# Layer 2 of a four-layer model: the context product once a sequence, two groups' maxima turned over together, and filler work dealt out by matmul passes

## The chip, the cores and the metric

The kernel runs on one core of one Trainium2 chip. The metric is the device time of one execution in microseconds (us), as the median of the runs; lower is better. The changed lines all belong to layer 2 (and to the constants packed for it); layers 0, 1 and 3 keep their code.

## The reference, cut to what matters

Activations are `x`, 8 sequences (B) of 512 tokens (T) of 128 channels (C), float32. Each layer computes `x = x + attn(LN(x)) * silu(ffn(LN(x)))`. Layer 2 is:

```
# attention side, per sequence
qkv   = LN(xn; g_attn, b_attn) @ qkv_w + qkv_b          # 16 heads of width 8
attn  = causal softmax attention(q, k, v)
attn  = attn @ out_w + out_b
x     = xn + attn
ctx   = attn
xs, vs = LN(x; g1, b1), 0
for _ in range(8):                                       # NUM_ITERS
    u  = tanh(ctx @ w_ctx + xs @ w_x + b_inl)
    vs = vs + 0.1 * (u - xs - vs)
    xs = xs + 0.1 * vs
x = x + xs
h = gelu(LN(x; g2, b2) @ ff_w1 + ff_b1)
s = x + (h @ ff_w2 + ff_b2)
# ffn side, per sequence
h = silu(xn @ w1) * (xn @ w2)
h = gelu(h @ h1);  h = gelu(h @ h2)                      # 512 x 512 each
g = h @ w3
# together
x = x + s * silu(g)
```

`ctx @ w_ctx` does not change over the eight iterations.

## The kernel before

Data stand in SBUF with 128 rows. A tile of 128x512 holds one sequence, either by tokens or by features. Products over a whole sequence are matmuls of 128x128 weights and 512 columns in float32; one such product is called a *pass* here.

Layer 2 walks over 128 *units*: 8 sequences, 4 head groups `g` in each, and 4 key chunks `kc` of 128 keys (`JT = 4`). A group has four heads. It lies on four 32-row strips, so that its four narrow matmuls go to different strips of the array. A sequence is 16 units. For one unit there are three pieces of attention work:

- **W**, `weights`: the scores of one key chunk against the queries from that chunk on (512, 384, 256 or 128 columns for `kc` = 0 to 3), into two PSUM tiles `pu` of two banks each, and their exponential on ScalarE (ACT) into `at`, two heads to an instruction (L1411).
- **M**, `maxima`: the row maxima of the scores of one query tile, which are needed some units later. The same two `pu` tiles take the scores, four bf16 products with `ident_b` and `neg_b` add the causal mask (L1390), and VectorE (DVE) reduces them (L1393) into `mpad`. `put_maxima` turns a whole group's maxima over with four transposes and adds them into `qT` (L1400, L1401), where a column of -1 in the keys subtracts them from the scores.
- **S**, `sums`: two units later (`LAG`), the product of the exponentials with the values, into the single `pf` bank (L1424).

Both W and M use both `pu` tiles, so W, exponentials, M, reductions and the next W follow one another.

Between these pieces the loop of `layer2` deals out other work, as generators whose steps end at each `yield`. *Front* is what the next sequence needs: `begin` (layer norm, projections to q, k, v) and `ffn` (the whole ffn side: four steps of two passes for w1 and w2 at L1348 and L1349, one step of 16 passes for h1, one of 16 for h2, both at L1361 with a Gelu on ACT for each four passes at L1362, and w3 at L1368). *Back* is what the finished groups need: `group` (transposing and normalising a group's output, L1438; after the last group the output projection and `ctx`), then `rest` (layer norm, eight iterations with two passes each at L1474 and L1475, Tanh at L1477, updates of the state at L1479 to L1482, layer norm, the 512-wide feed-forward at L1498 and L1504). A step is taken at fixed places:

```
held[u] = L.weights(*units[u])
next(back, None)
...
next(front, None)
if u + AHEAD < len(units):
    L.maxima(*units[u + AHEAD])
next(back if u % 2 else front, None)
```

The maxima run `AHEAD = 5` units ahead. The order of TensorE (PE) is the order in which the code issues its work (`manual_schedule`); the other engines' orders are set by the framework's scheduler. All evacuations of front and back go through three one-bank PSUM tiles `pa`.

The functions the change touches, with those that call them:

Of the kernel before, what the change touches and what calls it, by code (L numbers as in the profile page):

```python
# [10 lines left out]
F32 = mybir.dt.float32  # L11
# [1158 lines left out]
def pack2(i):  # L1170
# [10 lines left out]
    p.add("own", one)  # L1181
    bq, bk = (strips2(b[None, n * C : (n + 1) * C]).reshape(2, P).T for n in range(2))
# [4 lines left out]
    bk[16::32] = -1.0  # L1187
    p.add("bk", bk)
# [58 lines left out]
class Layer2(BySequence):  # L1247
# [39 lines left out]
    def begin(self, b):  # L1287

        k, nc, cn, tp = self.k, self.k.nc, self.cn, self.tp
# [13 lines left out]
        yield  # L1303
        q["xT"] = tp.tile([P, T], F32, name="xT2", bufs=1)
        k.to_features(xn, q["xT"], nt=JT)
        yield
# [4 lines left out]
        yield  # L1311
        q["qT"] = tp.tile([P, 4, T], F32, name="qT2")
        q["kT"] = tp.tile([P, 2, T], F32, name="kT2")
        for t in range(2):
# [13 lines left out]
            yield  # L1328
# [8 lines left out]
        yield  # L1337

    def ffn(self, b):
# [5 lines left out]
        for o in range(4):  # L1345
# [8 lines left out]
            yield  # L1354
        for n in ("h1", "h2"):
            src, hA = hA, hid()
            for o in range(4):
                ps = k.pa()
                for i in range(4):
                    c0 = i * FF2 + o * P  # L1360
                    nc.tensor.matmul(ps, fn[n][:, c0 : c0 + P], src[:, i, :], start=(i == 0), stop=(i == 3))  # L1361
                nc.scalar.activation(hA[:, o, :], ps, AF.Gelu, scale=fn[n + "_s"][:, o : o + 1])  # L1362
            yield
# [9 lines left out]
        yield  # L1373
# [7 lines left out]
    def maxima(self, b, g, qt):  # L1381
        k, nc, q = self.k, self.k.nc, self.q[b]
        qT, kT = q["qT"][:, g, :], q["kT"][:, g // 2, :]
# [7 lines left out]
        for i, pu in pairs:  # L1391
            top = self.mpad[g % 2][:, qt, :].rearrange("p (i c) -> p i c", c=32)
            nc.vector.tensor_reduce(top[:, i : i + 2, 16], pu[:, :, 0:m], AX.X, ALU.max)  # L1393

    def put_maxima(self, b, g):

        k, nc, qT = self.k, self.k.nc, self.q[b]["qT"][:, g, :]
        ps = k.pa((P, JT, P))
        for t in range(JT):
            nc.tensor.transpose(ps[:, t, :], self.mpad[g % 2][:, t, :], k.ident)  # L1400
        nc.vector.tensor_tensor(qT, qT, ps.rearrange("p a b -> p (a b)"), ALU.add)  # L1401
# [30 lines left out]
    def group(self, b, g):  # L1432
# [11 lines left out]
        yield  # L1444
# [4 lines left out]
        yield  # L1449
# [6 lines left out]
        q["ctx"] = tp.tile([P, T], F32, name="ctx2")  # L1456
        nc.scalar.activation(q["ctx"], ps, AF.Identity, bias=self.out_bc, scale=100.0)
        yield

    def rest(self, b):  # L1460
# [6 lines left out]
        yield  # L1467
        yield
        k.to_features(h, X[0], nt=JT, scale=self.g1[:, 0:1], bias=self.g1[:, 1:2])
        yield  # L1470
        for it in range(ITERS):
            now, then = X[it % 2], X[1 - it % 2]
            ps = k.pa()
            nc.tensor.matmul(ps, cn["w_ctx"], q["ctx"], start=True, stop=False)  # L1474
            nc.tensor.matmul(ps, cn["w_x"], now, start=False, stop=True)  # L1475
            u = tp.tile([P, T], F32, name="u2")
            nc.scalar.activation(u, ps, AF.Tanh, bias=cn["b_inl"], scale=0.01)  # L1477
# [5 lines left out]
            yield  # L1483
# [6 lines left out]
        yield  # L1490
        yield
        k.to_features(h, hT, nt=JT, scale=cn["g2"], bias=cn["b2"])
        nc.gpsimd.tensor_tensor(xn, xn, bc(cn["ff_b2"], 1, JT), ALU.add)
        yield
# [5 lines left out]
        yield  # L1500
# [16 lines left out]
        yield  # L1517


def layer2(k, x, A, at):  # L1520

    with ExitStack() as ctx:
# [7 lines left out]
        AHEAD = JT + 1  # L1530
        for u in range(AHEAD):
            L.maxima(*units[u])
        for _ in L.ffn(0):
            pass
        L.put_maxima(0, 0)
        U = 4 * JT
        front = back = iter(())
        for u in range(len(units) + LAG):
# [3 lines left out]
            next(back, None)  # L1542
            if n == 1 and b + 1 < B:
                front = chain(L.begin(b + 1), L.ffn(b + 1))
            if u % JT == JT - 1 and u + 1 < len(units):
                L.put_maxima(*units[u + 1][0:2])
            next(front, None)
            if u + AHEAD < len(units):
                L.maxima(*units[u + AHEAD])
            next(back if u % 2 else front, None)  # L1550
            if u >= LAG:
                wb, g, kc = units[u - LAG]
                L.sums(wb, g, kc, held.pop(u - LAG))
                if kc == JT - 1:
                    back = chain(L.group(wb, g), back)
                    if g == 3:
                        back = chain(back, L.rest(wb))
        for _ in back:
            pass
# [574 lines left out]
```

## Time and profile before

| what | value |
|---|---|
| median of 3 runs | 3675.19 us (3669.09 to 3679.26) |
| the profiled execution | 3659.7 us, of which the span from first to last instruction is 3658.0 us |
| mean granted TensorE clock | 0.831 |
| PE busy in the span | 2812.2 us (77%) |
| DVE, ACT, POOL busy | 2265.6 us (62%), 1643.1 us (45%), 783.7 us (21%) |
| layer 2, from its first layer norm to the last work of its last sequence | about 1472 to 2653 us of the span |

A profile row names the line, engine, operation, output and inputs, how often it occurs, busy time and mean duration, and the idle time of the engine just before it with what ended that. PE records of a float32 product come in two halves, so 64 records of L1361 are 32 passes. "PEclk" is the share of its full clock that TensorE was granted. Matmul durations contain the time in the pipeline, so that back-to-back matmuls overlap in the record.

### The profile page before, as it was taken

The numbers are of one execution on the slowest core, as the hardware profiler recorded it, in microseconds if no ns is written. First come the engines' busy times: TensorE is split into PE (matmuls) and PEld (weight loads), VectorE is DVE, ScalarE is ACT, GpSimd is POOL, SyncE is SP. The second block draws the span as 40 slices with busy tenths as digits, with TensorE's granted clock in tenths as the row PEclk, the third lists the DMA queues.
The fourth block names the chain that finished last, engine by engine and source line by source line (L and its number), as shares of the span: only waits on it lengthen the run. The fifth ranks groups of instructions, "written<-read, shape, count | busy, mean of one in ns | idle before, by whom it ended". The sixth has DMA issues, their size and how long they took to land.

```text
span 3658.0 us, 45079 instructions
## 1 busy us (share of the span) xinstructions
PE 2812.2 (77%) x16390; PEld 1510.1 (41%) x16390; DVE 2265.6 (62%) x6274; ACT 1643.1 (45%) x3211; POOL 783.7 (21%) x915
## 2 busy tenths in 40 slices
PE   6164657512988888699999999998668789887987
PEld 4142445302444444344444444444344445444543
DVE  7989898997581121334445445444467777777775
ACT  5163546512544445233333333333245566666665
POOL 0004040400226664201101101101122222222220
PEclk8585757555899999799998998998878899888987
DMA  4002030311002221100000000000000000000000
GB/s 119 2 2 71 1 81 1 72 48 34 1 10 45 38 38 24 58 1 1 1 1 1 1 1 1 1 1 1 18 3 1 4 4 1 4 4 4 1 4 6
DMA packets 67519, 64.53 MB, mean 18 GB/s; under 512 B 5344, under 2 KB 59616, under 8 KB 66784
## 3 DMA queue, kind: packets, MB, share of 16 engines
q1 hardware_dynamic: 39264, 42.75, 3.7%
q0 software_dynamic: 19712, 14.69, 2.9%
q10 hardware_dynamic: 8320, 4.19, 0.4%
q8 instruction: 129, 2.11, 0.2%
q14 instruction: 94, 0.77, 0.1%
HBM read 43.80 MB, written 17.83 MB: 17 GB/s over the span
## 4 chain that ended last, share of the span: by engine, by line
PE 45%; DVE 32%; ACT 13%; POOL 4%; issue 3%; DMA 1%; ACTq 0%; POOLq 0%; SPq 0%; DVEq 0%
PE pa L1361 6%; PE pu L1379 6%; DVE nm L1949 4%; ACT at L1950 4%; PE pu L1066 2%; PE pf L1086 2%; PE pu L1946 2%; DVE mpad L1393 2%; PE pf L1424 2%; DVE Z L700 2%; PE pf L1931 1%; PE pa L1475 1%; PE pa L1474 1%; PE pa L1000 1%; DVE Z L706 1%
## 5 line engine op out<-in xcount | busy, mean ns | idle before, releaser
L1950 ACT ACTIVATE at<-pu,nm 128x512 f32<-128x512 f32 x512 | 347.7, 687 | 145.9 <-DVE nm L1949 115.6
L199 POOL TENSOR_SCALAR_AFFINE_SELECT at<-at 128x512 f32<-128x512 f32 x256 | 187.2, 751 | 1030.4 <-ACT at L1411 856.9
L1949 DVE TENSOR_REDUCE nm<-pu 128x1 f32<-128x512 f32 x512 | 326.4, 679 | 66.8 <-PE pu L1946 66.7
L1393 DVE TENSOR_REDUCE mpad<-pu 128x2 f32<-128x256 f32 (+3 forms) x256 | 199.0, 817 | 169.1 <-PE pu L1390 169.1
L1411 ACT ACTIVATE at<-pu 128x1024 f32<-128x1024 f32 (+3 forms) x256 | 171.6, 701 | 286.3 <-PE pu L1379 286.1
L1071 ACT ACTIVATE at<-pu,rsqrt 128x1024 f32<-128x1024 f32 (+3 forms) x256 | 190.4, 791 | 225.3 <-PE pu L1066 221.8
L1946 PE MATMUL pu<-qT,kT 32*128 32x512 f32 x1024 | 247.6, 700 | 6.4 <-ACT at L1950 5.4
L1361 PE MATMUL pa<-hid,f 128*128 128x512 f32 x512 | 222.7, 593 | 0.0
L1379 PE MATMUL pu<-qT,kT 32*128 32x512 f32 (+3 forms) x1024 | 161.4, 518 | 56.5 <-DVE mpad L1393 41.8
L748 PE MATMUL pa<-ident,Y 128*128 128x128 f32 x32 | 7.9, 424 | 216.3 <-DVE Y L739 216.3
L1379 PE MATMUL pu<-kT,qT 32*128 32x128 f32 (+3 forms) x1024 | 152.1, 571 | 14.3 <-ACT at L1411 10.2
L548 POOL DMA_INDIRECT xg<-xn_d,idx x48 | 53.1, 1106 | 503.9 <-PE pf L552 321.8
L1931 PE MATMUL pf<-at,va 128*32 128x512 f32 x1024 | 156.4, 687 | 1.4 <-POOL va L1924 1.4
L1361 PEld LDWEIGHTS pa<-hid,f 128*128 128x128 f32 x512 | 96.6, 190 | 119.5 <-issue 118.9
L1086 PE MATMUL pf<-at,va 128*32 128x512 f32 (+3 forms) x1024 | 106.1, 490 | 42.1 <-POOL at L199 41.8
L1482 DVE SCALAR_TENSOR_TENSOR X<-X,u 128x512 f32<-128x512 f32 x56 | 38.6, 690 | 159.5 <-ACT u L1477 159.5
L1066 PE MATMUL pu<-qT,kT 32*128 32x512 f32 (+3 forms) x1024 | 130.5, 520 | 5.9 <-ACT at L1071 4.9
L1924 POOL TENSOR_TENSOR va<-V,sm 128x32 f32<-128x32 f32 x128 | 38.4, 300 | 450.4 <-DVE sm L1923 399.7
L1379 PEld LDWEIGHTS pu<-qT,kT 32*128 32x128 f32 x1024 | 67.8, 198 | 155.1 <-DVE mpad L1393 115.6
L1946 PEld LDWEIGHTS pu<-qT,kT 32*128 32x128 f32 x1024 | 82.2, 208 | 103.2 <-ACT at L1950 65.5
L1009 POOL DMA_INDIRECT f_d<-ys,idx x64 | 101.2, 1582 | 95.7 <-DMA f_d<-ys,idx 51.4
L1362 ACT ACTIVATE hid<-pa,f 128x512 f32<-128x512 f32 x64 | 44.0, 687 | 172.6 <-PE pa L1361 172.6
(608 smaller groups left out, 6606.4 us busy)
## 6 DMA issues: line engine op xcount, KB each, us to landing
w<-in_w_dram SPq DMA_DIRECT2D x24, 512.0 KB, 3.3
f_d<-zeros ACTq DMA_DIRECT2D x8, 512.0 KB, 6.0
xn_d<-xn SPq DMA_DIRECT2D x8, 512.0 KB, 3.6
w<-in_w_dram SPq DMA_DIRECT2D x16, 256.0 KB, 2.8
w<-in_w_dram SPq DMA_DIRECT2D x24, 128.0 KB, 2.1
f<-in_f_dram SPq DMA_DIRECT2D x1, 2888.0 KB, 11.8
xn<-in_x_dram SPq DMA_DIRECT2D x4, 512.0 KB, 7.5
Gt<-in_x_dram SPq DMA_DIRECT2D x4, 512.0 KB, 3.9
```

The source lines that it names most:

```text
L199: self.nc.gpsimd.affine_select(a, a if src is None else src, pattern, ALU.is_ge, 0.0, base=0, channel_multiplier=-1)
L1066: nc.tensor.matmul(pu[:, n, 0:m], q["kT"][r, g // 2, kc * P : kc * P + P], q["qT"][r, g, kc * P :], start=True, stop=True,)
L1071: nc.scalar.activation(at_[:, i : i + 2, 0:m], pu[:, :, 0:m], AF.Square, bias=k.rsqrt2, scale=32.0**-0.5)
L1086: nc.tensor.matmul(po[i * 32 : i * 32 + 32, kc * P :], va[:, kc, c0 : c0 + 32], at_[:, i, 0 : T - kc * P], start=(kc == 0), stop=(kc == JT ...
L1361: nc.tensor.matmul(ps, fn[n][:, c0 : c0 + P], src[:, i, :], start=(i == 0), stop=(i == 3))
L1379: self.k.nc.tensor.matmul(pu[:, n, 0:m], a[r, c0 : c0 + P], b[r, q0 : q0 + m], start=True, stop=stop)
L1393: nc.vector.tensor_reduce(top[:, i : i + 2, 16], pu[:, :, 0:m], AX.X, ALU.max)
L1411: nc.scalar.activation(at_[:, i : i + 2, 0:m], pu[:, :, 0:m], AF.Exp, scale=8.0**-0.5)
L1931: nc.tensor.matmul(po[i * 32 : i * 32 + 32, :], va[:, kc, c0 : c0 + 32], E[:, i, :], start=(kc == 0), stop=(kc == JT - 1))
L1946: nc.tensor.matmul(pu, q["kT"][r, kc * P : (kc + 1) * P], q["qT"][r, g, :], start=True, stop=True)
L1949: nc.vector.tensor_reduce(nm[:, w], pu, AX.X, ALU.max, negate=True)
L1950: nc.scalar.activation(E[:, n, :], pu, AF.Exp, bias=nm[:, w], accum_out=sm[:, w])
```

## The change

It does five things.

1. `ctx @ w_ctx` is made once a sequence, in a new last step of `group`, and copied to SBUF by ACT. An iteration multiplies by `w_x` alone; DVE adds the stored product to the PSUM result, into `u`, and the Tanh then reads `u`.
2. Maxima of two groups share one `mpad` tile: the second group's go to the next column (17). `put_maxima` works once for two groups: four transposes, then for each group one DVE operation that multiplies by a new 0/1 column (`put`) and adds to that group's `qT`. The keys get a second column of -1.
3. Maxima run nine units ahead (`AHEAD = PAIR + 1`), and take the query tile `(n - 1) % JT` for unit index `n`, so that M's width grows over a group while W's shrinks.
4. Every step of front and back says how many passes it holds (`yield 4.0`). h1 and h2 give up their turn after each four passes rather than after sixteen. A new function `fill`, called twice a unit, takes one step of back and then as many steps of front as a budget allows: 1.8 passes a call in the first sequence, 2.43 later. `begin` of the next sequence goes ahead of what is left of the present one's `ffn`.
5. S comes directly after W, ahead of both fills; and the first sequence's `ffn` is dealt out between the first nine maxima.

```diff
     def ffn(self, b):
...
                 nc.scalar.activation(hA[:, o, :], ps, AF.Gelu, scale=fn[n + "_s"][:, o : o + 1])
-            yield
+                yield 4.0
...
     def maxima(self, b, g, qt):
...
-            top = self.mpad[g % 2][:, qt, :].rearrange("p (i c) -> p i c", c=32)
-            nc.vector.tensor_reduce(top[:, i : i + 2, 16], pu[:, :, 0:m], AX.X, ALU.max)
+            top = self.mpad[g // 2][:, qt, :].rearrange("p (i c) -> p i c", c=32)
+            nc.vector.tensor_reduce(top[:, i : i + 2, 16 + g % 2], pu[:, :, 0:m], AX.X, ALU.max)
...
-    def put_maxima(self, b, g):
+    def put_maxima(self, b, t):
...
-        for t in range(JT):
-            nc.tensor.transpose(ps[:, t, :], self.mpad[g % 2][:, t, :], k.ident)
-        nc.vector.tensor_tensor(qT, qT, ps.rearrange("p a b -> p (a b)"), ALU.add)
+        for qt in range(JT):
+            nc.tensor.transpose(ps[:, qt, :], self.mpad[t][:, qt, :], k.ident)
+        top = ps.rearrange("p a b -> p (a b)")
+        for v in range(2):
+            to = qT[:, 2 * t + v, :]
+            nc.vector.scalar_tensor_tensor(to, top, put[:, v : v + 1], to, ALU.mult, ALU.add)
...
     def group(self, b, g):
...
-        q["ctx"] = tp.tile([P, T], F32, name="ctx2")
-        nc.scalar.activation(q["ctx"], ps, AF.Identity, bias=self.out_bc, scale=100.0)
-        yield
+        ctx = tp.tile([P, T], F32, name="ctx2", bufs=1)
+        nc.scalar.activation(ctx, ps, AF.Identity, bias=self.out_bc, scale=100.0)
+        yield 2.25
+        ps = k.pa()
+        nc.tensor.matmul(ps, cn["w_ctx"], ctx, start=True, stop=True)
+        q["ctx"] = tp.tile([P, T], F32, name="cw2")
+        nc.scalar.copy(q["ctx"], ps)
+        yield 1.0
...
     def rest(self, b):
...
-            nc.tensor.matmul(ps, cn["w_ctx"], q["ctx"], start=True, stop=False)
-            nc.tensor.matmul(ps, cn["w_x"], now, start=False, stop=True)
+            nc.tensor.matmul(ps, cn["w_x"], now, start=True, stop=True)
             u = tp.tile([P, T], F32, name="u2")
-            nc.scalar.activation(u, ps, AF.Tanh, bias=cn["b_inl"], scale=0.01)
+            nc.vector.tensor_tensor(u, ps, q["ctx"], ALU.add)
+            nc.scalar.activation(u, u, AF.Tanh, bias=cn["b_inl"], scale=0.01)
...
 def layer2(k, x, A, at):
...
-        AHEAD = JT + 1
+        U = 4 * JT
+        PAIR = 2 * JT
+        AHEAD = PAIR + 1
+        HALF = (1.8, 2.43)
...
+        def fill():
+
+            nonlocal credit
+            half = HALF[u >= U]
+            credit = min(credit, half) + half - next(back, 0.0)
+            while credit > 0.0:
+                passes = next(front, None)
+                if passes is None:
+                    break
+                credit -= passes
+
         for u in range(len(units) + LAG):
             b, n = divmod(u, U)
             if u < len(units):
                 held[u] = L.weights(*units[u])
-            next(back, None)
-            if n == 1 and b + 1 < B:
-                front = chain(L.begin(b + 1), L.ffn(b + 1))
-            if u % JT == JT - 1 and u + 1 < len(units):
-                L.put_maxima(*units[u + 1][0:2])
-            next(front, None)
-            if u + AHEAD < len(units):
-                L.maxima(*units[u + AHEAD])
-            next(back if u % 2 else front, None)
+                if u % PAIR == PAIR - 1 and u + 1 < len(units):
+                    L.put_maxima(units[u + 1][0], units[u + 1][1] // 2)
             if u >= LAG:
                 wb, g, kc = units[u - LAG]
                 L.sums(wb, g, kc, held.pop(u - LAG))
...
+            if n == LAG - 1 and b + 1 < B:
+                front = chain(L.begin(b + 1), front, L.ffn(b + 1))
+            fill()
+            if u + AHEAD < len(units):
+                maxima(u + AHEAD)
+            fill()
```

## The prediction

> **What bounds the kernel now.** The profiled execution took 3659.7 us (3658.0 of span), 15.5 under the median of the runs; sums are made on it and carried to the median. First the page's slices: layer 2 lies in slices 17 to 29.
>
> ```profile
> PE   6164657512988888699999999998668789887987
> ...
> DVE  7989898997581121334445445444467777777775
> ...
> PEclk8585757555899999799998998998878899888987
> ```
>
> PE reads 9 of 10 there and DVE 3 to 5. Then the table of stretches: one steady sequence (columns: length, PE, PEld, DVE, ACT, POOL busy, clock), the unit that holds h1 and h2, and two thin stretches.
>
> ```profile
> 1804.10:1941.20 137.10, 128.66 (x717) 61.16 (x716) 65.15 (x105) 50.15 (x73) 18.26 (x23) 0.94 0.00 1
> ...
> 1860.50:1893.60 33.10, 33.10 (x100) 14.27 (x100) 2.93 (x5) 10.59 (x14) 0.63 (x1) 1.00 0.00 1
> 1920.48:1930.72 10.24, 8.32 (x50) 3.40 (x48) 6.82 (x14) 2.30 (x4) 3.37 (x4) 0.67 0.00 0
> 1944.94:1958.59 13.65, 10.87 (x56) 5.23 (x52) 7.98 (x17) 4.02 (x6) 6.29 (x6) 0.59 0.01 1
> ```
>
> PE looks 94% busy. The chain of waits corrects that: h1's 16 passes (32 records) take 13.73 us.
>
> ```profile
> 1862.28 13.73 PE pa L1361 x32
> ```
>
> A pass is therefore 0.858 us. Counting a sequence's work in passes by columns (front 50, back 30, W, M and S 10, 11 and 10, turned maxima 2; four strips count as one) gives 113, or 97 us of 137. The other 40 go to waits along W, exponential, M, reduction, W, and to about 20 us a sequence at half clock in units with little to fill. The exponentials' starts (L1411) show it: of the third sequence's units (counted from 0), 8 took 33.1 us with all of h1 and h2, 4 to 7 and 9 to 12 took 4.4 to 8.5; units 1, 13 and 14, with 1.8 to 3.1 passes in all, took 6.2 to 7.2.
>
> The waits of that sequence confirm it:
>
> ```profile
> PEld pu L1379 <- DVE mpad L1393: 15.0, 17, 1.9
> ...
> PEld pu L1379 <- ACT at L1411: 6.4, 12, 1.0
> ```
>
> **The change, part by part: what goes.** Of 64 context products 56 go: 56 x 0.858 = 48 us of PE. Of 128 maxima transposes 64 go, an eighth of a pass each: 7 us. DVE's operations for the maxima keep number and size (32 at 682 ns). The constants' load grows by 1 KB on SP's queue, long before use: nothing. POOL's selects and powers keep their number.
>
> **What comes.** 64 DVE additions of 128x512 from PSUM (nearest row: L1401, 682 ns) are 44 us of an engine that is under half busy; they matter only inside the iteration. And ACT changes table more often. The built order of ACT holds 143 table loads before and 233 after: 44 more ahead of h1's and h2's Gelus, one ahead of the 512-wide feed-forward's, and 45 more ahead of exponentials, because Gelus and exponentials now alternate. The timeline shows what one costs:
>
> ```profile
> 1937.98 0.69 ACT L1499 ACTIVATE hid<-pa,c 128x512 f32<-128x512 f32 x1 [0.17 <-PE pa L1498]
> 1939.88 1.28 ACT L1411 ACT_TABLE_LOAD   x1 [1.21 <-PE pu L1379]
> 1941.17 1.02 ACT L1411 ACTIVATE at<-pu 128x1024 f32<-128x1024 f32 x1
> ```
>
> The load to exponentials doesn't run in the 1.21 us that ACT idles: it stands behind the wait for W, so 1.28 us go between W and its exponentials, then to M (which needs `pu`). The load to Gelu starts at once and hides behind its four passes. So of 115 us of loads (90 x 1.283) the exponentials' half, 58 us, can be exposed, where less than about 1.5 us are dealt between W and M.
>
> Here the Trainium skill speaks against the change: "ScalarE: Activation LUTs" (Table sets: the hidden batching unit) says to batch calls by table set, and its section on the cost of a load counts 1283 ns plus a drain of 1380 ns for each switch. The trace agrees on the load and shows no drain (0.01 us to the exponential). With the page's 2.66 us the 45 exposed at most would be an estimated 120 us.
>
> **A unit, by rows.** W takes 1.14, 0.93, 0.71, 0.50 us for chunks 0 to 3, its two exponentials 2.04, 1.62, 1.20, 0.76, the reductions 0.42, 0.68, 0.95, 1.22 each (maxima widths run opposite now), the mask 0.4, S 1.06 to 0.43. From a W to the next W: M starts when both the dealt passes and the exponentials are done; the next W when both the second fill and the first reduction are. Each evacuation that a following product needs stalls it 0.7 to 0.8. On units 4 to 12 of the third sequence of before the rule gives 5.6, 5.4, 7.6, 8.5, 32.7, 10.3, 4.3, 7.0, 4.8 = 86.2 us; the trace has 86.0.
>
> I lay the new order out the same way for its fourth sequence (97 passes). Three of its units: the first has nothing between W and M and a load: 1.14 + 0.1 + 1.28 + 1.8 + 0.1 to M, 0.65 for M and mask, then four passes of h2, 3.5: 8.6. The seventh holds two iterations and two passes of w1/w2: it waits for the chain (below): 9.0. The thirteenth holds nothing and a load: 5.7. All sixteen: 8.6, 5.4, 6.6, 7.9, 8.6, 4.7, 9.0, 8.0, 8.0, 8.0, 10.2, 10.3, 5.7, 7.2, 7.5, 8.6 = 124.3. Of the seven loads to exponentials in them five lie open. Four of the six steady sequences hold 101 passes: 4 x 0.858 x 4/6 = 2.3 more, 126.6. Before, these six took 824.4 us, 137.4 each. So 10.8 x 6 = **-65 us**.
>
> **Half clock.** The rule assumes full clock. Before, the half clock set in around units whose passes fill 22 to 39% of their time (1.8 passes in 7.2 us, 3.1 in 6.7). New holes of that kind: the units with no fill and a load on chunk 0 leave PE idle 2.5 us; one or two a sequence. The step then dealt, up to four passes, takes up to 3.4 us more. I take 2 us a sequence, **+12**, from bounds of 0 and 7 (two steps).
>
> **First and last parts.** First sequence: 111 by the rule against 116.5: **-5**. Ahead of it, nine maxima between the ffn's steps in place of five alone: bare maxima took 14 us for five, the ffn 42; the new stretch is 51 passes, 44 us, with some 6 for cold start and stalls: 50 plus the W against 56: **-4** (0 to -9). Last sequence to its last S: it takes over some 30 passes of ffn that earlier ones leave, 99 us by the rule, against 99.6: **0** (-6 to +8). The tail runs the last iterations alone, and there the change costs. Before:
>
> ```profile
> 2620.54 1.13 PE L1475 MATMUL pa<-X,c 128*128 128x512 f32 x2 [0.65 <-DVE X L1482]
> 2621.51 1.02 PE L1474 MATMUL pa<-ctx,c 128*128 128x512 f32 x2
> 2621.71 0.69 ACT L1477 ACTIVATE u<-pa,c 128x512 f32<-128x512 f32 x1 [1.94 <-PE pa L1475]
> 2622.43 0.69 DVE L1482 SCALAR_TENSOR_TENSOR X<-X,u 128x512 f32<-128x512 f32 x1 [1.14 <-ACT u L1477]
> ```
>
> The context product ran behind Tanh, at no cost to the period of 2.63 us. The addition stands in the chain: +0.75 (0.69 and a handover), 3.38. And PE's share falls from 65% to 25%, among the shares that went cold before: at half clock the product takes 1.91 rather than 1.13 us (it did at 2606.6), a period of 4.2. So +6 to +12, taken near the cold end by those shares: **+10**.
>
> "TensorE: Matmul & The Clock Gate" (Why this matters for your kernels) warns of gaps of over some 3 us between bursts; the gaps here would be about 2.2, so by its letter the clock holds and the sum is 4 us lower. No row shows a lone product in such a period.
>
> In the steady part the same chain is 2.3 us without handovers between product and product; two iterations a unit, with exponentials and reductions of the same unit in the same in-order queues: behind the addition's wait on DVE stand the reductions that release `pu`, for which W waits; behind Tanh the exponentials. That is in the 9.0 and 8.0s above. If every one of the 64 waited 1 us more it would be +64: the upper bound; the lower is nothing.
>
> Sum: -65 + 12 - 5 - 4 + 0 + 10 = **-52** us; 3675 - 52 = 3623, taken as **3625**.
>
> **Rivals.**
> *The waits eat the gain.* All exponentials' loads open (two more a sequence, 2.6 us) and 0.5 us for each iteration: 8 x 2.6 = 21 and 64 x 0.5 = 32, which leaves +1: 3676. For it: ACT and DVE are strictly in order. Against: h-steps dealt between W and M cover the loads.
> *Slower, by the clock.* The dealt-out steps meet holes again and again: if PE runs 20 us a sequence at half clock as before, but now in units filled with passes, each loses half of that, 10 us: 8 x 10 = 80 instead of 12; -52 + 68 = +16: 3691. It decides from about 18 us a sequence at half clock. For it: 56 passes of filler are gone and loads open holes; against: units without passes were the cold ones, and now nearly every unit has some.
> *PE nearly full.* Every unit as the dense ones of before, 1.6 us and 0.858 a pass: 16 x 1.6 + 100 x 0.858 = 111 a sequence, -155 in the six: 3520 or so. Against: iterations and loads.
> *It isn't dealt as said.* PE's order is written by the code, and the built order shows h1 and h2 in fours with W between them; only that the first nine maxima hide could fail, 4 us.
>
> **How the numbers follow.** A measurement of this kernel tells about 0.3%, 11 us, from no change. Forecast 0.58; its own range has the clock at 0 to 7 us a sequence, the first part at 0 to -9, the last at -6 to +8 and the tail at +6 to +12: 3596 to 3669; waits eat it 0.16, of which 0.06 is still faster and 0.10 the same; clock 0.18; PE nearly full 0.08. So faster 0.72, same 0.10, slower 0.18. The range 3570 to 3684 takes in the forecast and the waits, reaches some way towards PE nearly full, which it leaves out, and leaves out rather more than half of the clock's case.
>
> **What would show it.** The unit of 33 us should be gone and units lie between 4.7 and 10.5; sequences about 127 to 130 us; 233 table loads, 45 of the new ones behind waits for W; the tail's period near 3.4 to 4.2 us; less than 10 us a sequence at half clock. Wrong it is if sequences stay over 135 us, if DVE's reductions wait for Tanh for over 1 us in most iterations, or if PEclk in layer 2 falls below 0.9.

## The result, and the profile after

The changed kernel takes 3780.3 us (3777.0 to 3786.5, four runs) against 3677.2 for the kernel before beside it: a ratio of 1.028, with the 95% interval [1.0265, 1.0304]. It is 103 us slower where 52 less were forecast, and lies outside the stated range of 3570 to 3684. The profiled execution took 3778.4 us (3776.5 of span). Its slices, in tenths, as shown of before:

```profile
PE   6173757406888895988888878888658798788987
...
DVE  7889898995661223325445354443457777777775
...
PEclk9585858555899997989889888888768898888987
```

In layer 2 PE mostly reads 8 where it read 9, and the clock falls to 8 and in places 7 where it stood at 9. The table of stretches gives the fourth sequence (columns as before: length, PE, PEld, DVE, ACT, POOL busy, clock), then a cold and a full-speed stretch of it:

```profile
1987.70:2135.10 147.40, 122.39 (x675) 56.33 (x676) 71.38 (x113) 61.39 (x81) 18.70 (x23) 0.90 0.00 1
2080.30:2087.20 6.90, 6.10 (x11) 3.00 (x12) 3.14 (x4) 0.00 (x0) 0.02 (x1) 0.51 0.01 2
2115.00:2135.00 20.00, 17.74 (x92) 6.69 (x94) 5.59 (x6) 10.11 (x12) 1.27 (x2) 1.00 0.00 0
```

PE has 122 us of records in 147, and a tenth of the clock is missing. Part by part, from first exponential to first exponential (the steady sequences are the second to the seventh):

| part | before, us | after, us | difference | forecast |
|---|---|---|---|---|
| first maximum's reduction to first exponential | 56.0 | 50.0 | -6.0 | -4 |
| first sequence | 116.5 | 136.1 | +19.6 | -5 |
| six steady sequences | 824.4 | 888.4 | +64.0 | -65, and +12 for the clock |
| last sequence, to its last exponential | 84.6 | 114.3 | +29.7 | 0 for the last sequence, to its last sums |
| from there to the last work of layer 2 | 71.3 | 72.4 | +1.1 | +10 for the tail |

The last two rows divide a stretch that the forecast cut at the last sums; cut there, they are +16.5 and +14.2. (Another 10 us of the 119 between the two profiled executions lie ahead of layer 2, in layers 0 and 1, whose instructions keep their order.) The six steady sequences again, as two whole stretches, before and after:

```profile
1669.40:2493.80 824.40, 773.38 (x4264) 364.82 (x4265) 385.94 (x618) 300.72 (x432) 105.82 (x135) 0.94 0.00 1
```

```profile
1693.00:2581.50 888.50, 752.86 (x4076) 344.83 (x4076) 425.45 (x667) 376.70 (x494) 110.42 (x136) 0.89 0.00 1
```

PE's records shrink by only 20 us though 74 passes, 63 us, went from these six sequences: 42 context products, and 32 passes of ffn (28 of h1 and h2, 4 of w3) that now run in the last sequence, where none stood before. The reason seen in the trace is that more of the rest runs at half clock: by the clock's records 198 us of the 888, before 106 of 824. So the six are 64 us longer with less work in them. PE's idle time grows from 51.0 to 135.6 us. The table of waits says for whom; columns: engine, tile and line waiting, what ended it, us in total, times, longest. Before:

```profile
PE pu L1379 <- DVE mpad L1393: 34.9, 52, 1.7
PE pu L1379 <- ACT at L1411: 14.1, 30, 1.2
PE pa L1438 <- DVE oT L122: 1.6, 6, 0.3
```

After, the five longest of nine rows:

```profile
PE pu L1390 <- ACT at L1426: 33.9, 38, 1.9
PE pu L1390 <- DVE mpad L1405: 29.8, 45, 1.9
PE pa L1453 <- ACT oT L120: 25.0, 12, 3.6
PE pa L1494 <- DVE X L1502: 23.0, 23, 2.1
PE pa L1453 <- DVE oT L122: 11.6, 12, 2.0
```

Waits for the reductions shrink a little. New are 36.6 us in which a group's transposes wait for the copy of its sums (`oT`, 24 times, 1.5 us each), 23.0 us in which an iteration waits for the state of the one before, and 19.8 us more for exponentials. The timeline shows how idle time, table loads and clock meet (start, duration, engine and line; in brackets the idle time before it):

```profile
2074.78 1.28 ACT L1426 ACT_TABLE_LOAD   x1 [1.71 <-PE pu L1390]
...
2076.72 0.30 PEld L1390 LDWEIGHTS pu<-kT,qT 32*128 32x128 f32 x4 [1.35 <-ACT at L1426]
...
2081.10 1.12 PE L168 MATMUL pa<-ident,hr 128*128 128x128 f32 x4 [2.65 <-DVE hr L1229]
...
2082.01 6.19 PE L1372 MATMUL pa<-hid,f 128*128 128x512 f32 x8
```

W's exponentials wait for W, then for the load; M waits for them; the transposes dealt next wait 2.65 us for a layer norm; and then four passes of h take 6.19 us, at half clock. With no such hole ahead of it the same step takes 3.65:

```profile
2120.92 3.65 PE L1372 MATMUL pa<-hid,f 128*128 128x512 f32 x8
```

### The profile page after: what moved, and what is told of

The parts are those of the page before. It is cut to its first block, busy times and chain, and to the rows that moved or that the text cites. A ratio compares the mean times of both kernels' runs of the same rounds, so it can differ in the third digit from the quotient of the medians.

```text
span 3776.5 us, 44845 instructions
## 1 busy us (share of the span) xinstructions
PE 2819.6 (75%) x16214; PEld 1503.5 (40%) x16214; DVE 2317.3 (61%) x6338; ACT 1761.5 (47%) x3309; POOL 792.1 (21%) x915
## 3 DMA queue, kind: packets, MB, share of 16 engines
q8 instruction: 127, 2.08, 0.2%
## 4 chain that ended last, share of the span: by engine, by line
PE 33%; DVE 17%; ACT 10%; POOL 3%; issue 3%; DMA 1%; POOLq 0%; ACTq 0%; DVEq 0%; SPq 0%
PE pa L1372 7%; PE pu L1390 5%; DVE nm L1992 4%; ACT at L1993 4%; PE pu L1989 2%; PE pa L1494 2%; ACT at L1426 2%; DVE mpad L1405 2%; PE pf L1439 1%; PE pf L1974 1%; ACT L1426 1%; PE pa L1902 1%; DVE rope L1895 1%; PE pa L1947 1%; PE pa L1379 1%
## 5 line engine op out<-in xcount | busy, mean ns | idle before, releaser
L1405 DVE TENSOR_REDUCE mpad<-pu 128x2 f32<-128x1024 f32 (+3 forms) x256 | 199.1, 820 | 287.1 <-PE pu L1402 286.9
L1372 PE MATMUL pa<-hid,f 128*128 128x512 f32 x512 | 267.1, 671 | 0.0
L1390 PE MATMUL pu<-qT,kT 32*128 32x512 f32 (+3 forms) x1024 | 152.0, 517 | 45.6 <-DVE mpad L1405 40.4
L1372 PEld LDWEIGHTS pa<-hid,f 128*128 128x128 f32 x512 | 108.1, 220 | 141.6 <-issue 140.4
L1390 PE MATMUL pu<-kT,qT 32*128 32x512 f32 (+3 forms) x1024 | 131.4, 519 | 37.3 <-ACT at L1426 37.0
L1066 PE MATMUL pu<-qT,kT 32*128 32x512 f32 (+3 forms) x1024 | 129.7, 518 | 5.9 <-ACT at L1071 4.9
L1494 PE MATMUL pa<-X,c 128*128 128x512 f32 x128 | 90.7, 797 | 46.4 <-DVE X L1502 43.2
L1989 PEld LDWEIGHTS pu<-qT,kT 32*128 32x128 f32 x1024 | 81.8, 208 | 102.8 <-ACT at L1993 63.7
```

The source lines that it names most:

```text
L1066: nc.tensor.matmul(pu[:, n, 0:m], q["kT"][r, g // 2, kc * P : kc * P + P], q["qT"][r, g, kc * P :], start=True, stop=True,)
L1390: self.k.nc.tensor.matmul(pu[:, n, 0:m], a[r, c0 : c0 + P], b[r, q0 : q0 + m], start=True, stop=stop)
L1405: nc.vector.tensor_reduce(top[:, i : i + 2, 16 + g % 2], pu[:, :, 0:m], AX.X, ALU.max)
L1494: nc.tensor.matmul(ps, cn["w_x"], now, start=True, stop=True)
L1989: nc.tensor.matmul(pu, q["kT"][r, kc * P : (kc + 1) * P], q["qT"][r, g, :], start=True, stop=True)
```

## First experiments: single parts

**Sums later.** The changed kernel with S moved behind the second fill.

```diff
-            if u >= LAG:
-                wb, g, kc = units[u - LAG]
-                L.sums(wb, g, kc, held.pop(u - LAG))
...
                 maxima(u + AHEAD)
             fill()
+            if u >= LAG:
+                wb, g, kc = units[u - LAG]
+                L.sums(wb, g, kc, held.pop(u - LAG))
...
```

> The changed kernel with S put back behind the second fill (its place before the change); all else as changed. Theory S (sums directly after W leave the group's transposes at the head of PE with the evacuation of the sums still to run; the trace shows 36.6 us of PE idle on that evacuation in the six steady sequences, 1.6 before): those stalls go, with the ends about 45 us, so about 3735, and more if half clock shrinks with them. Theory L (table loads) and theory C (the iteration's longer chain): nothing much, 3770 to 3790, since the loads (235) and the iterations stay; a stall that moves to the next place would also give that.

Measured: 3748.5, ratio 1.0196 [1.0179, 1.0213]: 32 less than the change. In the six steady sequences the wait for `oT` fell from 36.6 to 3.8 us and that for the reductions from 29.8 to 14.7, but another rose:

```profile
PE pu L1390 <- ACT at L1426: 53.4, 39, 2.4
```

The sums had covered exponentials; they now cover reductions. The direction holds; the size is under that expected: the six sequences took 851.3 us in place of 888.4.

**No table changes for h.**

```diff
-                nc.scalar.activation(hA[:, o, :], ps, AF.Gelu, scale=fn[n + "_s"][:, o : o + 1])
+                nc.scalar.activation(hA[:, o, :], ps, AF.Tanh, scale=fn[n + "_s"][:, o : o + 1])
```

> The changed kernel with Tanh in place of Gelu after h1 and h2 alone, which shares its table with the exponentials: 130 table loads rather than 233, the same passes and the same order of PE. It computes another function there. Theory L: the loads open between W and its exponentials and the half clock that follows them are most of the loss, 60 to 90 us, so 3690 to 3720, and the first sequence, which has no iterations, falls from 136 to about 115 us. Theory S or C: the exponentials' waits are 34 us in six sequences against 14 before, so 25 us at most, 3755 to 3780.

Measured: 3706.8, ratio 1.0076 [1.0059, 1.0093]: 73 less. In the six sequences (836.2 us) M's and W's waits for exponentials fell by 11 us only, but time at half clock fell from 198 to 130, which is up to 34 us of lost work. So here the loads cost more through the clock than by the waits behind them. The first sequence fell to 128.7 us, not to the 115 that theory L expected. This looked like the main cause; the kernels at fixed places, below, limit that.

**Context product in each iteration again** (changed kernel otherwise).

```diff
+            nc.tensor.matmul(ps, cn["w_ctx"], q["ctx"], start=True, stop=False)
-            nc.tensor.matmul(ps, cn["w_x"], now, start=True, stop=True)
+            nc.tensor.matmul(ps, cn["w_x"], now, start=False, stop=True)
...
-            nc.vector.tensor_tensor(u, ps, q["ctx"], ALU.add)
-            nc.scalar.activation(u, u, AF.Tanh, bias=cn["b_inl"], scale=0.01)
+            nc.scalar.activation(u, ps, AF.Tanh, bias=cn["b_inl"], scale=0.01)
```

> The changed kernel with the context product in each iteration again (two products, no addition on DVE), at the same places in PE's order; 56 passes more. Theory C: PE's waits for the state (23 us in six sequences, 14 + 6 in the last and the tail) go, the tail's period falls from 4.34 to 2.63 us (14 us), the passes add up to 48 us: net about -10 to +10 in the steady part and -14 in the tail, 3755 to 3785; if half clock falls with the denser PE, down to 3740. Theories L and S: the passes come on top, +25 to +35: 3805 to 3815.

Measured: 3769.1, ratio 1.0254 [1.0237, 1.0271]: 56 passes more, and 11 us faster, as theory C said. By the profile the end behind the last exponential is 14 us shorter and the six steady sequences are 6.5 longer.

**Context product once, on the kernel before**: the same edit the other way round.

> The kernel before with the first part of the change alone: context product once a sequence, added on DVE. If passes set the time in the steady sequences it gains 56 x 0.858 = 48 us less about 14 in the tail: 3645. Theory C: each iteration's chain is 0.75 us longer and lies open, and PE gets colder: +10 to +40, 3690 to 3715. Theories L and S say nothing of it beyond that it is not the loss: 3640 to 3680.

Measured: 3699.2, ratio 1.0058 [1.0041, 1.0075]: 21 us slower with 56 passes less. The forecast's 48 us of removed work are worth nothing: in the six sequences PE's records fell by 30 us and its idle time grew by 38 (51.0 to 88.6); the six took 7 us more, last sequence and tail 18.5. (The edit also gives `group` one step more, so that what follows in back comes a place later; that was not varied by itself.)

## Second round: what adds, and h in fours

**Sums later and no table changes**, both edits above.

> The changed kernel (3780) with both edits that helped alone: the sums moved behind the second fill (-32 alone) and Tanh in the place of the Gelus after h1 and h2 (-73 alone), so that these two layers compute another function and ACT loads 130 tables instead of 233. If the two causes are separate (evacuations that the group's transposes wait for, table loads ahead of exponentials), the effects add: 3675, 3665 to 3690, level with the kernel before. If both mostly work through the same half clock, they overlap: 3690 to 3705. What would still be missing against the forecast (3625), 50 us or more, would then belong to the iteration's chain and to the tail.

Measured: 3656.6, ratio 0.9947 [0.993, 0.9963]. This lies below both ranges: the two are worth 124 together, more than the 105 of their sum. By the profiles the six steady sequences do add up (-37 and -52 alone, -91 together), and so does their time at half clock (-58 and -68 alone, -116 together, to 82 us). Most of the surplus lies in the first sequence: 136.1 us in the change, 129.4 and 128.7 with one edit, 107.8 with both; at half clock it ran 44.4, 37.5, 41.0 and 6.8 us. There one edit alone leaves the clock low, and only both together keep it up.

**h1 and h2 whole, sums later.**

```diff
-                yield 4.0
+            yield 16.0
```

> The changed kernel with the sums behind the second fill (3748 alone) and h1 and h2 kept whole, 16 passes a step, counted as 16 in the budget; Gelus stay. 159 table loads instead of 235. Theory loads: the 103 loads that Tanh took away were worth 73 us, 0.71 each; 76 fewer give -54: 3695 (3680 to 3710). Rival, splitting is right and only the table was costly: a block of 16 passes drives the budget far below nothing, units after it get no front work and go to half clock: 3720 to 3750.

Measured: 3755.5, ratio 1.0208 [1.0191, 1.0225]. The rival holds, 5 us above its range: 76 loads fewer brought nothing. By the loop's arithmetic a block of 16 leaves the credit far below nothing and the units behind it without front work. Time at half clock in the six sequences is 164 us, against 140 with fours.

**h in fours on the kernel before**, at its fixed places.

```diff
-            yield
+                yield
```

(the second stands within the loop over `o`)

> The kernel before (3677) with one edit: h1 and h2 give up their turn after each four passes, dealt at the fixed places of before; 199 table loads instead of 143. Theory loads: 56 more at 0.71 us are +40, 3717 (3700 to 3735). Rival, spreading: the passes reach the thin units behind h, which ran at half clock, and the loads hide: 3640 to 3675.

Measured: 3644.5, ratio 0.9909 [0.9893, 0.9926]: 35 us faster with 56 more loads. "Loads cost 0.7 each" falls. Before, units 8 to 12 of a sequence took 33.1, 8.2, 4.4, 7.8 and 4.9 us (58.4); here 12.5, 9.3, 10.6, 10.2 and 11.2 (53.8): the passes now cover waits of thin units. In the six sequences the weight loads of the scores (PEld) wait 106.1 us for reductions and exponentials, where they waited 131.5.

**The maxima's parts alone on the kernel before**: pairs, `AHEAD` of nine, opposite widths, the ffn between the first maxima.

```diff
-        AHEAD = JT + 1
+        AHEAD = PAIR + 1
...
-            if u % JT == JT - 1 and u + 1 < len(units):
-                L.put_maxima(*units[u + 1][0:2])
+            if u % PAIR == PAIR - 1 and u + 1 < len(units):
+                L.put_maxima(units[u + 1][0], units[u + 1][1] // 2)
```

> The kernel before with the parts of the change that concern the maxima alone: two groups turned over together, nine units ahead, their widths running opposite to W's, and the first sequence's ffn dealt between the first nine maxima; context product in each iteration, h1 and h2 whole, fixed places, sums last. The stretch ahead of the first exponential was 5.9 us shorter in the changed kernel; 64 transposes fewer are at most 7 us. If those parts are as good as forecast: 3664 (3655 to 3671). Rival, opposite widths or the longer lead cost something (wide maxima stand beside narrow W's, where the reductions release the score banks later): 3677 to 3700.

Measured: 3657.2, ratio 0.9937 [0.9921, 0.9954]: 22 us faster, somewhat better than the forecast's -11 for them. By the profile some 9 lie in the last sequence with its tail and 3 in the steady six; the stretch ahead of the first exponential is 2.0 shorter, and 6.0 only once h runs in fours too.

So two parts of the change are good, and budget, sums' place and context product must cost more than the net loss.

## Third round: the budget

**Fours and maxima at fixed places**: both good parts, nothing else. In the loop, against the changed kernel (the fills alone are shown):

```diff
+            next(back, None)
...
+            next(front, None)
-            fill()
             if u + AHEAD < len(units):
                 maxima(u + AHEAD)
-            fill()
+            next(back if u % 2 else front, None)
```

> The kernel before with both parts that helped alone: h1 and h2 in fours (-35) and the maxima's parts (pairs, nine units ahead, opposite widths, the ffn between the first maxima: -22); context product in each iteration, sums last, steps at the fixed places of before; 199 table loads. Theory deal (the budget's placing of the steps, with its open table loads, is what costs): the parts are separate and add: 3677 - 35 - 22 = 3620, 3610 to 3635. Rival, both fill the same thin units: 3635 to 3650.

Measured: 3631.9, ratio 0.9877 [0.986, 0.9893]: the best of all, 47 us under the kernel before; 10 of the 57 overlap.

**The budget on top of that.**

> The changed kernel with the sums behind the second fill and the context product in each iteration: it differs from the run with fours and maxima at fixed places by the budget alone. 243 table loads. Theory deal: 3748 (sums late alone) less the 11 us of the context product: 3737, 3722 to 3748, some 115 above fixed places. Rival, the budget is harmless once sums and iteration are as before: 3620 to 3670.

Measured: 3686.7, ratio 1.0021 [1.0012, 1.0031]. The budget costs 55, not 115; so the context product in each iteration was worth 62 here, not 11. ("The budget" is the whole of `fill` with what goes with it: two steps of back a unit where fixed places give three in two units, the turned maxima ahead of the first of them, `begin` ahead of what is left of `ffn`. These were not varied apart.) By the profile the loss lies in the first sequence (129.4 us against 107.0), the steady six (824.3 against 805.9) and the last with its tail (164.6 against 145.5).

The first sequence holds the same passes of ffn in both, so there nothing is left for later; but M's waits for exponentials rise from 2.7 to 12.1 us, and time at half clock from 10.2 to 37.5. With sums last and the loads for h gone it took 107.8 under the same budget. From the steady six 24 passes of ffn, 21 us, move on to the last sequence; they lose 18 us in spite of it, and there too M waits for exponentials:

```profile
PE pu L1390 <- ACT at L1426: 51.0, 48, 2.4
```

against, at fixed places:

```profile
PE pu L1390 <- ACT at L1426: 15.6, 19, 1.7
```

Counting from the trace how often M waited over 0.7 us for exponentials that stood behind a load, in the six sequences: 0 of 35 with fours at fixed places; 28 of 48 with the budget; 13 of 42 in the changed kernel. At a fixed place every unit that deals h deals four passes between W and M, and the load runs beneath them. A budget whose credit is below nothing deals nothing there.

**Fours on the kernel before, with Tanh for the Gelus of h.**

> The kernel before with h1 and h2 in fours at fixed places (3644.5), and Tanh in the place of the Gelus after h1 and h2: another function, 128 table loads instead of 199. In the steady part of the run with Gelus none of 35 exponentials behind a load kept the next scores waiting over 0.7 us. Theory hidden loads (a load costs only where no passes stand between W and M): 3640, 3632 to 3646. Rival, each load costs 0.7 us wherever it stands: 71 fewer are -50: 3595, 3585 to 3610.

Measured: 3652.6, ratio 0.9928 [0.9911, 0.9944]. 71 loads fewer gain nothing: it is 8 us slower, and the steady six take 805.1 us, with Gelu 803.5. What a load costs is set by its place, not by its 1.28 us.

**The changed kernel with fixed places for the budget.**

> The changed kernel (3780) with the steps at the fixed places of before instead of the budget; sums directly after W, context product once, fours and maxima as changed. 199 table loads. Theory deal: the budget costs some 115 with sums late; here the same: 3665, 3640 to 3690. Rival, the sums' place and the iteration's chain carry the loss and the budget only repeats it: 3715 to 3760.

Measured: 3826.3, ratio 1.0397 [1.0379, 1.0414]: a miss for both. Without the budget it is worse, 194 above the best. So sums' place and context product together weigh more at fixed places (194) than under the budget (94).

## Fourth round: sums' place and context product apart

**Context product once, at fixed places, sums last.**

> Fours and maxima's parts at fixed places, sums last (3632), with the context product once a sequence and the addition on DVE. Theory chain (the addition lengthens each iteration, the tail's above all, whatever else is dealt): as on the kernel before, +21: 3653, 3645 to 3665. Rival, the price under the budget (3687 to 3748) holds here too: +62: 3694, 3680 to 3705.

Measured: 3640.0, ratio 0.9896 [0.988, 0.9913]: +8, below both ranges. The six sequences even gain 4 us (801.6); last sequence and tail lose 18.

**Sums directly after W, at fixed places**, context product in each iteration.

> Fours and maxima's parts at fixed places (3632), context product in each iteration, with the sums directly after W. Sums' place and context product together cost 194 at fixed places; less the 21 to 62 of the context product the sums' place is 132 to 173: 3764 to 3805. Rival, the two need each other and the sums' place alone is worth what it is under the budget, 82: 3714, 3700 to 3730.

Measured: 3772.1, ratio 1.0256 [1.0239, 1.0273]: +140 from this one edit. Its steady six take 925.8 us, 202 of them at half clock, and wait like this:

```profile
PE pu L1390 <- DVE mpad L1405: 78.2, 66, 4.7
PE pa L1453 <- ACT oT L120: 27.1, 12, 3.1
PE pa L1453 <- DVE oT L122: 10.3, 12, 0.9
PE pu L1390 <- ACT at L1426: 3.3, 6, 0.5
```

**The same with a group's steps joined later**, behind the unit's last place.

```diff
             if u >= LAG:
                 wb, g, kc = units[u - LAG]
                 L.sums(wb, g, kc, held.pop(u - LAG))
-                if kc == JT - 1:
-                    back = chain(L.group(wb, g), back)
...
             next(back if u % 2 else front, None)
+            if u >= LAG and kc == JT - 1:
+                back = chain(L.group(wb, g), back)
...
```

> The run with the sums directly after W at fixed places, where a finished group's steps (transposing its output first) are put into the queue only behind the unit's last place, so that they no longer follow the sums at once. Theory evacuation (the transposes wait for the copy of the sums' bank, in the changed kernel 36.6 us of 135.6 idle in six sequences): most of the price goes, 3640 to 3670. Rival, cover (the sums are missed behind the maxima, where they covered the reductions that the next W waits for): within 20 us of the run with the sums directly after W.

Measured: 3691.4, ratio 1.0041 [1.0027, 1.0055]. Both mechanisms are real: 81 of the 140 were the transposes that follow the sums at once (the `oT` rows are gone, time at half clock 120 us), and 59 are left, with the sums alone moved. Of these the missing cover of the reductions shows in the waits:

```profile
PE pu L1390 <- DVE mpad L1405: 74.0, 48, 4.3
```

With the sums last that row is 41.2, and time at half clock 96 us.

**A filler product in each iteration**, with the context product once at fixed places.

```diff
+            nc.tensor.matmul(ps, cn["w_ctx"], q["ctx"], start=True, stop=True)
             nc.tensor.matmul(ps, cn["w_x"], now, start=True, stop=True)
```

> The run with the context product once at fixed places, with one more product of the same size in front of each iteration's own; its result is overwritten, so the function is the same: PE has as many passes as with the product in each iteration, the chain keeps the addition on DVE. Theory chain: no gain on the run without it, 0 to +15. Theory clock (a lone product leaves PE too idle, and it falls to half clock): 8 to 25 us under the run without it, since in the tail at half clock the period was 4.35 instead of some 3.4, 7 us in eight iterations.

Measured: 3643.9, ratio 0.991 [0.9894, 0.9927], 4 us above the run without it, while its own runs go from 3625 to 3644. By the total theory chain's range holds and theory clock's doesn't; but the total hides two opposite effects, and the tail shows the clock's. One iteration of the changed kernel's tail:

```profile
2732.69 2.08 PE L1494 MATMUL pa<-X,c 128*128 128x512 f32 x2 [2.32 <-DVE X L1502]
2734.80 0.69 DVE L1496 TENSOR_TENSOR u<-pa,cw 128x512 f32<-128x512 f32 x1 [1.44 <-PE pa L1494]
2735.59 0.72 ACT L1497 ACTIVATE u<-u,c 128x512 f32<-128x512 f32 x1 [3.68 <-DVE u L1496]
2736.34 0.69 DVE L1502 SCALAR_TENSOR_TENSOR X<-X,u 128x512 f32<-128x512 f32 x1 [0.85 <-ACT u L1497]
```

and with the filler:

```profile
2594.32 1.13 PE L1495 MATMUL pa<-X,c 128*128 128x512 f32 x2 [1.47 <-DVE X L1503]
...
2595.28 1.02 PE L1494 MATMUL pa<-cw,c 128*128 128x512 f32 x2
```

The period is 2.63 us with the product in each iteration, 4.40 without, 3.45 with the filler. So the tail's 1.77 us an iteration are 0.82 for the addition in the chain and 0.95 for the clock, which is at half where PE has one product to do: the product takes 2.08 us, and 1.13 with the filler. The filler's passes cost the steady part what they save in the tail (806.9 against 801.6 us in the six, 76.9 against 83.7 in the tail).

## Last round

**The changed kernel with a group's steps joined later**: the same edit behind the second fill.

> The changed kernel (3780) with one edit: a finished group's steps join the queue behind the unit's second fill, so that the transposes no longer follow the sums at once. Sums still directly after W, budget, context product once. Theory evacuation: PE idled 36.6 us in six sequences before the transposes, 6.6 in the first and 7.8 in the last: 51 us at most, and some half clock with it: 3720 to 3740. Rival, the budget only moves the stall (as with the sums late, -32): 3745 to 3765.

Measured: 3754.1, ratio 1.0222 [1.0205, 1.0239]: -26. The rival holds: the `oT` rows (36.6 us) are gone, but the wait for exponentials rose from 33.9 to 43.6 us and that for reductions from 29.8 to 38.3. Under the budget half of what was filled opens again elsewhere. (The kernel before beside this run took 3671.9; by the ratios the gain is 23.)

**h spread further on the best version.**

```diff
-            next(back if u % 2 else front, None)
+            if u % 2 or n <= 8:
+                next(back if u % 2 else front, None)
```

> Fours and maxima's parts at fixed places (3632), but from the tenth unit of a sequence on the second front place is left out, so that h1 and h2 reach to units 14 and 15 instead of 12; 227 table loads. Theory spreading (thin units run at half clock; about 16 us a sequence at half clock are left): 3615 to 3628. Rival, hidden loads no longer all hide and the chain of fours only moves: 3630 to 3650.

Measured: 3633.1, ratio 0.9899 [0.9882, 0.9915], by the median as without it (3631.9), and in the rival's range. Beside its own kernel before (3671.9) it is even 0.2% behind, and its steady six take 812.7 us against 805.9. Time at half clock in the six is 99 us against 96: this spreading gains nothing.

All medians with fours and the maxima's parts, side by side:

| steps | sums | context product | us |
|---|---|---|---|
| fixed places | last | each iteration | 3631.9 |
| fixed places | last | once | 3640.0 |
| fixed places | after W | each iteration | 3772.1 |
| fixed places | after W | once | 3826.3 |
| budget | last | each iteration | 3686.7 |
| budget | last | once | 3748.5 |
| budget | after W | each iteration | 3769.1 |
| budget | after W | once (the change) | 3780.3 |

From the kernel before to the change, along one path: 3679 - 47 for fours and maxima, + 55 budget, + 62 context product once, + 32 sums' place. Along another path the same three parts cost 140, 54 and -46. They are not separate quantities: each opens holes, and what a hole costs depends on what else is there to fill it and on whether it brings the clock down. What holds along every path measured: the sums directly after W lose 32 to 186 us, the context product once loses 8 to 62.

## Why the prediction was wrong, by its own steps

**What was right.** The stretch ahead of the first exponential: -6.0 against -4. The tail: the addition's 0.82 us an iteration (forecast 0.75), a half clock, a product of 2.08 us (1.91); +14 us against +10, just over its bound of +12. A load of 1.283 us with no drain behind it: 43 loads ahead of exponentials took 55.2 us in the six sequences, and the exponential at 2076.07 began 0.01 us after its load. The unit of 33 us is gone. The prediction's own signs of being wrong came: sequences of 146 to 150 us, and PEclk below 0.9.

**The step that failed is the unit by rows, and the -65 built on it.** The six sequences were to gain 53 us with the clock's share and lost 64; the first was to gain 5 by the same rows and lost 19.6. For the fourth sequence the rows gave 124.3 us; it took 147.4. Unit by unit the excess is not even. The first three units were forecast at 8.6, 5.4 and 6.6 and took 8.5, 4.9 and 7.9; units 3, 9, 10 and 13 (counted from 0), forecast at 7.9, 8.0, 10.2 and 7.2, took 13.1, 11.8, 14.2 and 11.8. Together these four are 17.6 of the 23.1 us missed. In each, PE waits for something dealt too close to what it needs, and runs 3.4 to 7.7 us at half clock: for `xa` (the input of the projections), 1.9; for `oT` (the copy of a group's sums) before its transposes, 2.0 and 1.2; for `hr` (the output of a layer norm) before its transposes, 2.6.

Three terms behind that were mis-sized:

- *The sums' place was costed at nothing*: it was only listed among the rows of a unit. It costs 32 us in the change, and up to 186 at fixed places. What hid the copy of the sums' bank before was the next W, and the sums themselves hid part of the reductions; neither cover was named. The stalls for evacuations were counted at 0.7 to 0.8; those of the transposes took 1.5 each, 24 times.
- *Half clock*: 2 us a sequence, +12 in all. Time at half clock rose from 17.6 to 33.0 us a sequence, in units with passes; half of the 92 us added in the six sequences is up to 46 us of lost work there.
- *The removed context products* were counted at their full 48 us, and the iteration's waits as contained in the units. Removing them from the kernel before, alone, costs 21 us: PE's records fall by 30 us in the six and its idle time grows by 38. In the changed kernel it costs 11, with 23.0 us in the six in which PE waits for the state.

The loads were seen but priced by their length. Five open ones a sequence were reckoned in, some 38 us in the six, and 58 at most; M's waits behind them were 31 us there. But taking them away was worth 73 in all and 52 in the six, where time at half clock fell by 68 us (up to 34 us of lost work). In the first sequence, once the sums are last, they make 22 us (129.4 against 107.8). "Slower, by the clock" named the right mechanism and its condition (from 18 us a sequence; it was 33), but priced it 89 us too low, because it took the idle time itself as forecast. (The bounds of the forecast's own range add up to 3667 at the upper end, not 3669, which decides nothing.)

**What the Trainium skill says of this.** That calls should be batched by table set ("ScalarE: Activation LUTs", Table sets: the hidden batching unit) is borne out under the budget (-73 us without the table changes for h) and not at fixed places (71 loads fewer, +8 us). "TensorE: Matmul & The Clock Gate" (Why this matters for your kernels) warns of gaps over some 3 us; here the clock fell at 2708.4 with no gap over 2.33 us in the stretch of full clock ahead, and stayed at half through a whole tail with gaps of 2.32; it was full with gaps of 1.47. So the measurement decides. Its section on what is actually happening there describes windows of about 3.4 us; the trace agrees, as every half-clock stretch of layer 2 is a multiple of 3.4 us.

What stays open: why the context product once costs 62 us under the budget with the sums last and 54 at fixed places with the sums after W, but 8 and 11 in the other two pairs. In the pair of 62 the steady six take 27 us more and the last sequence with the tail 29, and PE waits 23.0 us for the state; that the budget can put two iterations into every unit was not varied by itself.

## What to carry to other kernels

Before moving a step in an interleaved order, list what it covers at its old place and what follows it at once at the new one; a step of under 1.1 us, moved past the others, cost 32 to 186 us here, where 56 removed matmul passes could give 48 at most. Cut long steps in pieces, but give each piece a place where it covers a named wait (with four passes between scores and maxima, none of 35 exponentials behind a table load kept the maxima waiting over 0.7 us), rather than letting a budget like this one choose. And work taken off an engine gains only where that engine sets the end; where it merely filled holes, its removal can also lower the clock for what is left.

## What the hardware showed unexpectedly

- A lone float32 product of 128x512 in a dependent chain, with gaps of 2.32 us, ran at half clock for all eight iterations (2.08 us, PEclk 0.50 from 2713.6 to 2744.4); with a second, useless product, and gaps of 1.47 us, the clock was full from the second iteration on (1.13 us), and the iteration was 0.95 us shorter.
- The clock comes down in steps of 3.4 us. The six steady sequences of the change hold 35 half-clock stretches of 3.4 to 10.2 us, those of the kernel before 12 of 6.8 to 13.7. A hole of 2.65 us (before 2081.10) was enough to have 6.9 us around it at half clock, and the passes dealt just behind paid for it: 6.19 us for four in place of 3.65.
